# Signed bfloat16 token numbers in the dispatch table of a mixture-of-experts kernel

## The chip, the cores and the metric

The kernel runs on one core of one Trainium2 chip. The metric is the device time of one execution in microseconds (us), from a few executions of the same program on the same chip; their median is the number that counts.

## What is computed

The reference is two transformer layers with post-layernorm over x of 8 batches x 512 tokens x 512 channels, all float32:

```
x = layernorm(x + attention0(x))      # 16 causal heads of 32
x = layernorm(x + experts(x))         # 8 experts, every token goes to its best two
x = layernorm(x + attention1(x))      # 8 query heads of 64 on 2 key/value heads
x = layernorm(x + quantised_ffn(x))   # hidden size 1408, integer weights
```

The part that matters here is between the first and the second line. A router takes the softmax of 8 logits of each token and picks the best two experts, so 8 x 512 x 2 = 8192 (token, expert) pairs have to be gathered by expert, multiplied with that expert's weights, and scattered back.

## The kernel before

**Stages.** TensorE (PE) goes through four stages in the order of the layers: attention0 batch by batch, the experts tile by tile (a tile is 128 tokens of one expert), attention1 batch by batch, and the feed-forward. Stages overlap at their seams. In attention0 the loop runs over batches `b`, head groups `g` (four) and units `u` (three per group); `plan(b)` hangs side work on the slots `(g, u)`: projections of the batch itself, and for batch `b - 1` its output projection `project` (`ps_o`), its layernorm and the store of its rows to the table `rows` in DRAM, and for batch `b - 2` the routing: `choose`, `dispatch`, then at slot (1, 2) `enter(one_hot(b - 2))`. So batches 0 to 5 are entered during the loop of b = 2 to 7, and batches 6 and 7 later, between the first steps of the expert tiles. The order is written by hand for PE through attention0 and the first expert steps; the other engines' order there is found by a scheduler. From the twelfth expert tile on the order of VectorE (DVE), ScalarE (ACT), GpSimd (POOL) and of the DMA queue of SyncE (SP) is by hand as well.

**The table of tiles.** `Router.table` is 128 lanes x 256 columns; column `32 e + j` is tile j of expert e, and the entry says which token sits in that lane. It is filled by a matrix product of one-hot matrices: for each of the 4 token tiles of a batch and each of the 2 choices, `one_hot` (L574) makes a 128x128 matrix that is zero but for the token's number at (token, lane), and a 128x256 matrix that has a one at (token, column); `enter` (L591) multiplies them on PE and adds the result to the table. A bfloat16 number holds whole numbers exactly only up to 256, and a token's number goes to 4095, so it is entered in two digits, `low` (the token's place in its tile of 128) and `high` (the number of that tile): two products, 2 x 8 matrices each time, accumulated in `ps_table[:, 0]` and `ps_table[:, 1]`, and put together by DVE at L597 and L598. `matmul_by_columns` (L58) issues each product as four of 32 output lanes (`columns=32`) in the loop of attention0, and as one of 128 in the two late calls. `ps_table` is one of two rotating PSUM banks (`p_mm`), which `ps_o`, `ps_q`, `ps_k`, `ps_v`, `rs`, `ps_count` and `ps_x1T` share.

**The rows.** `layernorm` (L180) stores the normalised batch with four DMAs of 128 rows to `router.rows[512 b + 128 t]`. The expert tiles gather rows from there with an indirect DMA on POOL's queue (L863), by the numbers in the table; `load_rows` (L1941) reads a whole batch back for attention1 with one DMA of 1 MB. Batches 0 and 1 are read back during the expert tiles, in SP's hand-written order; batches 2 to 7 together when attention1 begins.

**Round trip of the expert tiles.** From tile 18 on, a pair of gathered tiles is transposed by a way through DRAM: DVE transposes 32x32 blocks, SP stores the pair (`pair<-xrT`, L902) and reads it back in another order (`xrT<-pair`, L908), four DMAs, before PE needs it.

Of the kernel before, what the change touches and what calls it, by code (L numbers as in the profile page):

```python
# [9 lines left out]
F32 = mybir.dt.float32  # L10
# [4 lines left out]
ALU = mybir.AluOpType  # L15
# [3 lines left out]
P = 128  # L19
# [14 lines left out]
TOP_K = 2  # L34

E_TILES = NB * NT


FIXED, SOON = 6, 4
# [72 lines left out]
class Env:  # L112
# [67 lines left out]
    def layernorm(self, b, dst=None):  # L180
        nc, small = self.nc, self.small
        xb = self.xs[b]
        stats = small.tile([P, NT, 6], F32, name="stats")
        mv = small.tile([P, NT, 2], F32, name="mv")
        rstd = small.tile([P, NT], F32, name="rstd")
        for t in range(NT):
            nc.vector.bn_stats(out=stats[:, t, :], in_=xb[:, t, :])  # L187
            nc.vector.bn_aggr(out=mv[:, t, :], in_=stats[:, t, :])  # L188
        nc.gpsimd.tensor_scalar(rstd, mv[:, :, 1], LN_EPS, None, ALU.add)  # L189
        nc.gpsimd.tensor_tensor(rstd, rstd, self.neg_half, ALU.pow)  # L190
        for t in range(NT):
            nc.vector.tensor_scalar(xb[:, t, :], xb[:, t, :], mv[:, t, 0:1], rstd[:, t : t + 1],  # L192
                                    ALU.subtract, ALU.mult)
            if dst is not None:
                nc.sync.dma_start(out=dst[ts(t, P), :], in_=xb[:, t, :])

    def evacuate(self, i, dst, src):
        if i % 2:
# [166 lines left out]
def quantised_ffn(env, ffn_slots):  # L365
    tc, nc, xs, vec = env.tc, env.nc, env.xs, env.vec
    with ExitStack() as phase:
        work = phase.enter_context(tc.tile_pool(name="d_work", bufs=2))
        p_gu = phase.enter_context(tc.tile_pool(name="d_gu", bufs=2, space=PSUM))
        p_o = phase.enter_context(tc.tile_pool(name="d_o", bufs=1, space=PSUM))  # L370

        sd = work.tile([P, D], F32, name="sd", bufs=1)
        nc.sync.dma_start(out=sd, in_=env.ins.s_down.partition_broadcast(P))
        env.load_ffn(ffn_slots, 6)

        n_gu = 2 * NHID
        for i, slot in enumerate(ffn_slots):
            lo, hi = UPS * i, min(UPS * (i + 1), 3 * NHID)  # L380
            cut = min(max(n_gu, lo), hi) - lo
            if cut:
                nc.vector.tensor_scalar(slot[:, :cut, :], slot[:, :cut, :].bitcast(I32), -ZERO_POINT, None, ALU.add)
            n = hi - lo - cut
            if n:
                part = slot[:, cut : cut + n, :]
                nc.vector.scalar_tensor_tensor(part, part.bitcast(I32), -ZERO_POINT,
                                               sd[:, None, :].to_broadcast([P, n, D]), ALU.add, ALU.mult)

        def wf(u):  # L390
            return ffn_slots[u // UPS][:, u % UPS, :]

        for b in range(NB):
            xb = xs[b]
            x3T = work.tile([P, ND, S], F32, tag="x3T", name="x3T")
            env.transposed(x3T, xb, p_gu, "g")
            os = [p_o.tile([P, D], F32, tag=f"o{t}", name=f"ps_f{t}") for t in range(NT)]

            def ffn_out(c, hT):
                for t in range(NT):  # L400
                    nc.tensor.matmul(os[t], lhsT=hT[:, ts(t, P)], rhs=wf(n_gu + c), start=c == 0, stop=c == NHID - 1)

            before = None
            for c in range(NHID):
                g = p_gu.tile([P, S], F32, tag="g", name="ps_g1")
                u = p_gu.tile([P, S], F32, tag="u", name="ps_u1")
                for ps, w in ((g, wf(2 * c)), (u, wf(2 * c + 1))):
                    for dc in range(ND):
                        nc.tensor.matmul(ps, lhsT=w[:, ts(dc, P)], rhs=x3T[:, dc, :], start=dc == 0, stop=dc == ND - 1)
                sg = work.tile([P, S], F32, tag="sg", name="sg1")  # L410
                nc.scalar.activation(sg, g, AF.Silu, scale=vec[:, V_SG + c : V_SG + c + 1])
                hT = work.tile([P, S], F32, tag="hT", name="hT2", bufs=3)
                nc.vector.scalar_tensor_tensor(hT, u, vec[:, V_SU + c : V_SU + c + 1], sg, ALU.mult, ALU.mult)
                if before is not None:
                    ffn_out(c - 1, before)
                before = hT
            ffn_out(NHID - 1, before)
            for t in range(NT):
                nc.vector.tensor_tensor(xb[:, t, :], os[t], xb[:, t, :], ALU.add)
            env.layernorm(b, env.ins.out[b])  # L420

class Router:
# [4 lines left out]
    def __init__(self, env, keep, pool, small, tmp, dram):  # L429
        nc = env.nc  # L430
        self.env, self.nc, self.keep, self.small = env, nc, keep, small
        self.results = dram.tile([(N_FIXED + N_FREE) * P, D], F32, name="results")
        self.rows = dram.tile([NB * S, D], F32, name="rows")
        n = NB * NT
        self.hots = pool.tile([P, TOP_K, n, E], F32, name="r_hots")
        self.weights = keep.tile([P, TOP_K, n], F32, name="r_weights")
# [29 lines left out]
        self.tiles = numbers("r_tiles", [N_FREE], [[1, N_FREE]])  # L466
        i = tmp.tile([P, 1], I32, name="r_lane_i")
        nc.gpsimd.iota(i, pattern=[[0, 1]], base=0, channel_multiplier=1)
        self.lane = pool.tile([P, 1], F32, name="r_lane")
        nc.vector.tensor_copy(self.lane, i)  # L470
        i = tmp.tile([P, S], F32, tag="r_inv", name="r_columns_i", bufs=2)[:, : E * E_TILES].bitcast(I32)
        nc.gpsimd.iota(i, pattern=[[1, E * E_TILES]], base=0, channel_multiplier=0)
        self.columns = pool.tile([P, E * E_TILES], BF16, name="r_columns")
# [100 lines left out]
    def one_hot(self, b, room, tiles):  # L574


        nc, n = self.nc, TOP_K * NT
        room = room.rearrange("p c t -> p (c t)").bitcast(BF16)
        low = room[:, : n * P].rearrange("p (i l) -> p i l", l=P)
        high = room[:, n * P : 2 * n * P].rearrange("p (i l) -> p i l", l=P)  # L580
        column = room[:, 2 * n * P :].rearrange("p (i l) -> p i l", l=E * E_TILES)
        lanes = self.columns[:, :P]
        for k, t in ((k, t) for t in tiles for k in range(TOP_K)):
            i, lane = TOP_K * t + k, self.to_lane[:, k, t : t + 1]
            nc.vector.tensor_scalar(low[:, i, :], lanes, lane, self.lane, ALU.is_equal, ALU.mult)
            nc.vector.tensor_scalar(high[:, i, :], lanes, lane, float(NT * b + t), ALU.is_equal, ALU.mult)
            nc.vector.tensor_scalar(column[:, i, :], self.columns, self.to_column[:, k, NT * b + t : NT * b + t + 1], None,
                                    ALU.is_equal)
        return low, high, column

    def enter(self, ps, low, high, column, columns):  # L591

        nc, n = self.nc, TOP_K * NT
        for h, part in enumerate((low, high)):
            for i in range(n):
                matmul_by_columns(nc, ps[:, h, :], part[:, i, :], column[:, i, :], i == 0, i == n - 1, columns)
        nc.vector.tensor_tensor(self.table, ps[:, 0, :], self.table, ALU.add)  # L597
        nc.vector.scalar_tensor_tensor(self.table, ps[:, 1, :], float(P), self.table, ALU.mult, ALU.add)  # L598

    def soon(self, pool, ps, held):  # L600

# [216 lines left out]
class Tiles:  # L818
# [39 lines left out]
    def fetch(self, i, room=None):  # L858
        if i < self.n:
            self.xrs[i] = xr = self.work.tile([P, D], F32, tag="xr", name="xr", bufs=6) if room is None else room  # L860

            n = (NB - 2) * S if i < self.n_soon else NB * S
            self.nc.gpsimd.indirect_dma_start(  # L863
                out=xr, out_offset=None, in_=self.router.rows[:n],
                in_offset=bass.IndirectOffsetOnAxis(ap=self.tokens(i), axis=0))
# [270 lines left out]
class IntegerFfn:  # L1136
# [102 lines left out]
    def batch(self, b):  # L1239
# [15 lines left out]
        if not final:  # L1255
            for t in range(NT):
                self.out(os, t, NHID - 1, parts[NHID - 1])
            for t in range(NT):
                self.scaled(b, os, t)
            env.layernorm(b, env.ins.out[b])  # L1260
            return

        order = [(t, c) for ts_ in ((0, 1), (2,), (3,)) for cs in (range(hold, NHID - 1), (NHID - 1,)) for t in ts_ for c in cs]
# [20 lines left out]
def attention0(env, guard, keep, routes, experts, dram, p_mm, tiles_ctx):  # L1284
# [8 lines left out]
    with ExitStack() as phase:  # L1293
# [37 lines left out]
        router = Router(env, keep, routes, small, work, dram)  # L1331
        router.load()
        load_x(0)

        for i in range(N_FIXED + N_FREE - RARE, N_FIXED + N_FREE):
            nc.sync.dma_start(out=router.results[ts(i, P), :], in_=guard.total)
# [48 lines left out]
        def project(b, t, out_of_heads=False):  # L1385
            ps = mm([P, D], "ps_o")
            for c in range(ND):
                (wide if out_of_heads else multiply)(ps, aoTs[b][:, c, ts(t, P)], wo[:, c, :], c)
            nc.vector.tensor_tensor(xs[b][:, t, :], ps, xs[b][:, t, :], ALU.add)
            if t == NT - 1:  # L1390
                env.layernorm(b, router.rows[S * b : S * (b + 1)])

        x1Ts, logits = {}, {}

# [45 lines left out]
            return router.one_hot(b, rooms[b], places)  # L1440

        def enter(rows, mm=mm, columns=HD):
            router.enter(mm([P, 2, E * E_TILES], "ps_table"), *rows, columns)

        def scores(b, g, u):
            q, k = heads[b, g]
# [481 lines left out]
def usual_pass(tc, ins, held_out):  # L1928
    nc = tc.nc
    with ExitStack() as ctx:  # L1930
# [4 lines left out]
        with tc.tile_pool(name="a_mm", bufs=2, space=PSUM) as p_mm, ExitStack() as attn1_ctx:  # L1935
            with tc.tile_pool(name="routes", bufs=1, side="right") as routes, \
# [2 lines left out]
                router, tiles, tables = attention0(env, guard, keep, routes, experts, dram, p_mm, tiles_ctx)  # L1939

                def load_rows(b):  # L1941
                    rows = router.rows[S * b : S * (b + 1)]
                    nc.sync.dma_start(out=env.xs[b], in_=rows.rearrange("(t p) d -> p t d", p=P))
# [333 lines left out]
```

## Time and profile before

| | |
|---|---|
| time, median of 3 executions | 2129.05 us (2126.14 to 2129.59) |
| the profiled execution, its time | 2131.2 us |
| its span, first to last instruction | 2129.5 us |
| PE busy | 2088.1 us, 98% of the span |
| DVE busy | 1278.1 us, 60% |
| ACT / POOL busy | 607.0 us, 29% / 497.9 us, 23% |
| granted TensorE clock, mean | 0.998 of full speed |
| HBM read and written | 129.96 MB and 75.76 MB, 97 GB/s over the span |

Busy time of an engine counts its instructions, overlapping ones once. The profiled execution is 2.15 us above the median of the three, and 1.7 us of its time lie outside its span. A line of a timeline gives the start, the duration, the engine, the source line, the operation with `output<-inputs`, and in brackets how long the engine was idle before and what ended that. On PE several entries of one duration overlap, since matmuls are pipelined.

### The profile page before, as it was taken

The numbers are of one execution on the slowest core, as the hardware profiler recorded it, in microseconds if no ns is written. First come the engines' busy times: TensorE is split into PE (matmuls) and PEld (weight loads), VectorE is DVE, ScalarE is ACT, GpSimd is POOL, SyncE is SP. The second block draws the span as 40 slices with busy tenths as digits, with TensorE's granted clock in tenths as the row PEclk, the third lists the DMA queues.
The fourth block names the chain that finished last, engine by engine and source line by source line (L and its number), as shares of the span: only waits on it lengthen the run. The fifth ranks groups of instructions, "written<-read, shape, count | busy, mean of one in ns | idle before, by whom it ended". The sixth has DMA issues, their size and how long they took to land. (4 is left out here: it accounts for less than half of the span.)

```text
span 2129.5 us, 36298 instructions
## 1 busy us (share of the span) xinstructions
PE 2088.1 (98%) x15322; PEld 1056.4 (50%) x15322; DVE 1278.1 (60%) x2015; ACT 607.0 (29%) x838; POOL 497.9 (23%) x489
## 2 busy tenths in 40 slices
PE   8999999999998999999999999999999999999997
PEld 2333333333333677775433333333334888888886
DVE  2667676676767644224237898888867644555443
ACT  2333323323333111111133333333332232222222
POOL 2343534334342211232042312322101000000000
PEclk9999999999999999999999999999999999999999
DMA  9020303415232337787651312132101311111000
GB/s 321 21 74 28 100 7 115 137 53 159 67 114 100 124 124 231 219 236 214 176 203 55 99 50 90 60 100 68 52 1 60 95 53 60 60 60 60 20 21 21
DMA packets 170444, 208.16 MB, mean 98 GB/s; under 512 B 61714, under 2 KB 114962, under 8 KB 167202
## 3 DMA queue, kind: packets, MB, share of 16 engines
q1 hardware_dynamic: 158992, 170.08, 25.8%
q0 software_dynamic: 10560, 34.61, 5.5%
q8 instruction: 123, 2.02, 0.4%
q10 hardware_dynamic: 722, 1.07, 0.1%
q14 instruction: 47, 0.39, 0.1%
HBM read 129.96 MB, written 75.76 MB: 97 GB/s over the span
## 5 line engine op out<-in xcount | busy, mean ns | idle before, releaser
L1460 ACT ACTIVATE p<-sc 128x2048 f32<-128x2048 f32 (+1 forms) x96 | 153.0, 1593 | 185.4 <-PE sc L62 161.8
L1068 POOL TENSOR_TENSOR g_total<-g_total,r_inv 128x512 f32<-128x512 f32 x64 | 90.1, 1408 | 491.0 <-DVE r_inv L1838 270.0
L1495 DVE TENSOR_TENSOR p<-p 128x1536 f32<-128x1536 f32 (+2 forms) x96 | 149.5, 1558 | 81.3 <-POOL p L1470 78.0
L1218 DVE SCALAR_TENSOR_TENSOR hT<-ps_u,vec,sg 128x512 f32<-128x512 f32 x88 | 65.5, 744 | 189.1 <-PE ps_u L1213 189.0
L1229 PE MATMUL ps_f<-ffn_w,h_half 128*128 128x512 f32 x672 | 169.9, 393 | 2.5 <-DVE h_half L1224 1.9
L948 PE MATMUL ps_gu<-xrT,experts 128*128 128x256 f32 x736 | 166.7, 380 | 1.0 <-DMA xrT<-pair 1.0
L948 PEld LDWEIGHTS ps_gu<-xrT,experts 128*128 128x128 f32 x736 | 138.9, 190 | 33.4 <-issue 15.1
L1808 ACT ACTIVATE p<-sc 128x1024 f32<-128x1024 f32 x128 | 124.7, 1022 | 98.2 <-PE sc L62 98.0
L1838 DVE RECIPROCAL r_inv<-r_inv 128x512 f32<-128x512 f32 x32 | 107.1, 3346 | 68.3 <-ACT r_inv L1065 68.3
L1229 PEld LDWEIGHTS ps_f<-ffn_w,h_half 128*128 128x128 f32 x672 | 124.4, 188 | 34.8 <-DVE h_half L1224 7.5
L1213 PE MATMUL ps_g<-x_high,ffn_w 128*128 128x512 f32 x352 | 137.3, 390 | 0.9 <-DVE x L1780 0.9
L1213 PE MATMUL ps_u<-x_high,ffn_w 128*128 128x512 f32 x352 | 137.1, 389 | 0.0
L1213 PE MATMUL ps_g<-x_low,ffn_w 128*128 128x512 f32 x352 | 137.0, 389 | 0.0
L1213 PE MATMUL ps_u<-x_low,ffn_w 128*128 128x512 f32 x352 | 137.0, 389 | 0.0
L62 PE MATMUL sc<-qT,kT 64*64 64x512 f32 x1024 | 124.7, 602 | 2.4 <-issue 1.3
L62 PE MATMUL ps_q<-experts 128*32 128x512 f32 x1024 | 121.5, 603 | 4.9 <-DMA experts<-in_xT 4.5
L1470 POOL TENSOR_SCALAR_AFFINE_SELECT p<-p 128x512 f32<-128x512 f32 x128 | 81.9, 652 | 167.7 <-ACT p L1460 161.1
L62 PE MATMUL ps_v<-experts 128*32 128x512 f32 x1024 | 120.9, 595 | 0.0
L1827 PE MATMUL av<-p,v 128*64 128x512 f32 x512 | 120.9, 594 | 0.0
L62 PE MATMUL ps_o<-attn_out,aoT 128*64 128x512 f32 x512 | 116.4, 598 | 0.8 <-ACT r_inv L1065 0.8
L62 PE MATMUL ps_k<-experts 128*32 128x512 f32 x1024 | 116.3, 594 | 0.0
L62 PE MATMUL ps_q<-hT,attn_qkv 128*64 128x512 f32 (+1 forms) x504 | 116.2, 596 | 0.0
(276 smaller groups left out, 3222.0 us busy)
## 6 DMA issues: line engine op xcount, KB each, us to landing
results<-y SPq DMA_DIRECT2D x68, 256.0 KB
turned<-turned SPq DMA_DIRECT2D x56, 256.0 KB
pair<-xrT SPq DMA_DIRECT2D x25, 512.0 KB
xrT<-pair SPq DMA_DIRECT2D x100, 128.0 KB
x<-in_x SPq DMA_DIRECT2D x8, 1024.0 KB
rows<-x SPq DMA_DIRECT2D x32, 256.0 KB
x<-rows SPq DMA_DIRECT2D x8, 1024.0 KB
experts<-in_xT SPq DMA_DIRECT2D x7, 1024.0 KB
```

What stands on the lines that cost most here:

```text
L62: nc.tensor.matmul(out[m], lhsT=lhsT[:, m], rhs=rhs, start=start, stop=stop)
L948: nc.tensor.matmul(ps[:, j, :], lhsT=w, rhs=xT[:, c, :], start=c == 0, stop=c == ND - 1)
L1068: self.nc.gpsimd.tensor_tensor(self.total, self.total, r_inv, ALU.add)
L1213: nc.tensor.matmul(ps, lhsT=w[:, ts(dc, P)], rhs=x[:, dc, :], start=(dc, i) == (0, 0), stop=(dc, i) == (ND - 1, 1))
L1218: nc.vector.scalar_tensor_tensor(hT, u, vec[:, V_SU + c : V_SU + c + 1], sg, ALU.mult, ALU.mult)
L1229: self.nc.tensor.matmul(os[t], lhsT=h[:, ts(t, P)], rhs=self.weights(2 * NHID + c), start=(c, i) == (0, 0), stop=(c, i) == (NHID - 1, 1))
L1460: nc.scalar.activation(p, sc[:, :, :width], AF.Exp, scale=scale)
L1470: nc.gpsimd.affine_select(out=first, in_=first, pattern=[[0, 4], [1, P]], compare_op=ALU.is_ge, fill=0.0, base=0, channel_multiplier=-1)
L1495: nc.vector.tensor_tensor(total[:, :, P * kt :], total[:, :, P * kt :], p[:, :, at : at + w], ALU.add)
L1808: nc.scalar.activation(p, sc, AF.Exp, scale=scale)
L1827: nc.tensor.matmul(st["av"][HD * j : HD * (j + 1), :], lhsT=st["v"][:, kt, HD * j : HD * (j + 1)], rhs=p[:, j, :], start=kt == 0, stop=kt ...
L1838: nc.vector.reciprocal(r_inv, r_inv)
```

## The change

A token enters the table as one number. Within a batch the token's number less 256 goes from -256 to 255; numbers from 0 on are raised by one, so that none is zero: -256 to -1 and 1 to 256, all exact in bfloat16. `held` is `513 b + 256` wherever the product isn't zero, and table + product + held is the token's row in DRAM. So that no decoding is needed, `rows` has 513 rows per batch, the one in the middle (number 256) unused. That row is written once with zeros, because the gather's range covers it. The value `held` is kept in the room in SBUF that `high` had. Tile t of a batch begins at `row_at(b, t)`; as the two halves of a batch no longer touch, `load_rows` takes two DMAs of 512 KB in place of one of 1 MB.

```
+GAP = S // 2
...
-                nc.sync.dma_start(out=dst[ts(t, P), :], in_=xb[:, t, :])
+                nc.sync.dma_start(out=dst(t), in_=xb[:, t, :])
...
-        self.rows = dram.tile([NB * S, D], F32, name="rows")
+        self.rows = dram.tile([NB * (S + 1), D], F32, name="rows")
...
+        self.signed = pool.tile([P, NT], F32, name="r_signed")
+        for t in range(NT):
+            nc.vector.tensor_scalar(self.signed[:, t : t + 1], lane, float(P * t - GAP + (P * t >= GAP)), None, ALU.add)
...
         for k, t in ((k, t) for t in tiles for k in range(TOP_K)):
             i, lane = TOP_K * t + k, self.to_lane[:, k, t : t + 1]
-            nc.vector.tensor_scalar(low[:, i, :], lanes, lane, self.lane, ALU.is_equal, ALU.mult)
-            nc.vector.tensor_scalar(high[:, i, :], lanes, lane, float(NT * b + t), ALU.is_equal, ALU.mult)
+            nc.vector.tensor_scalar(token[:, i, :], lanes, lane, self.signed[:, t : t + 1], ALU.is_equal, ALU.mult)
             nc.vector.tensor_scalar(column[:, i, :], self.columns, self.to_column[:, k, NT * b + t : NT * b + t + 1], None,
                                     ALU.is_equal)
...
-        for h, part in enumerate((low, high)):
-            for i in range(n):
-                matmul_by_columns(nc, ps[:, h, :], part[:, i, :], column[:, i, :], i == 0, i == n - 1, columns)
-        nc.vector.tensor_tensor(self.table, ps[:, 0, :], self.table, ALU.add)
-        nc.vector.scalar_tensor_tensor(self.table, ps[:, 1, :], float(P), self.table, ALU.mult, ALU.add)
+        for i in range(n):
+            matmul_by_columns(nc, ps, token[:, i, :], column[:, i, :], i == 0, i == n - 1, columns)
+        nc.vector.tensor_scalar(held, ps, 0.0, float((S + 1) * b + GAP), ALU.not_equal, ALU.mult)
+        nc.vector.tensor_tensor(self.table, ps, self.table, ALU.add)
+        nc.vector.tensor_tensor(self.table, held, self.table, ALU.add)
+
+    def row_at(self, b, t):
+        return (S + 1) * b + P * t + (P * t >= GAP)
...
-            n = (NB - 2) * S if i < self.n_soon else NB * S
+            n = (NB - 2 if i < self.n_soon else NB) * (S + 1)
...
+        nc.sync.dma_start(out=router.rows[GAP :: S + 1], in_=guard.total[:NB, :])
...
-            router.enter(mm([P, 2, E * E_TILES], "ps_table"), *rows, columns)
+            router.enter(mm([P, E * E_TILES], "ps_table"), *rows, columns)
...
                 def load_rows(b):
-                    rows = router.rows[S * b : S * (b + 1)]
-                    nc.sync.dma_start(out=env.xs[b], in_=rows.rearrange("(t p) d -> p t d", p=P))
+                    for t in range(0, NT, GAP // P):
+                        rows = router.rows[router.row_at(b, t) :][:GAP]
+                        nc.sync.dma_start(out=env.xs[b][:, t : t + GAP // P, :], in_=rows.rearrange("(t p) d -> p t d", p=P))
```

More of the change, by code (lines that the diff above doesn't have):

```diff
@@ L419, in quantised_ffn @@
                 nc.vector.tensor_tensor(xb[:, t, :], os[t], xb[:, t, :], ALU.add)
-            env.layernorm(b, env.ins.out[b])
+            env.layernorm(b, lambda t: env.ins.out[b][ts(t, P), :])
 class Router:
@@ L468, in __init__ @@
         nc.gpsimd.iota(i, pattern=[[0, 1]], base=0, channel_multiplier=1)
-        self.lane = pool.tile([P, 1], F32, name="r_lane")
-        nc.vector.tensor_copy(self.lane, i)
+        lane = pool.tile([P, 1], F32, name="r_lane")
+        nc.vector.tensor_copy(lane, i)
+        self.signed = pool.tile([P, NT], F32, name="r_signed")
+        for t in range(NT):
+            nc.vector.tensor_scalar(self.signed[:, t : t + 1], lane, float(P * t - GAP + (P * t >= GAP)), None, ALU.add)
         i = tmp.tile([P, S], F32, tag="r_inv", name="r_columns_i", bufs=2)[:, : E * E_TILES].bitcast(I32)
@@ L578, in one_hot @@
         room = room.rearrange("p c t -> p (c t)").bitcast(BF16)
-        low = room[:, : n * P].rearrange("p (i l) -> p i l", l=P)
-        high = room[:, n * P : 2 * n * P].rearrange("p (i l) -> p i l", l=P)
+        token = room[:, : n * P].rearrange("p (i l) -> p i l", l=P)
         column = room[:, 2 * n * P :].rearrange("p (i l) -> p i l", l=E * E_TILES)
+        held = room[:, n * P : 2 * n * P].bitcast(F32)[:, : E * E_TILES]
         lanes = self.columns[:, :P]
@@ L584, in one_hot, with enter @@
             i, lane = TOP_K * t + k, self.to_lane[:, k, t : t + 1]
-            nc.vector.tensor_scalar(low[:, i, :], lanes, lane, self.lane, ALU.is_equal, ALU.mult)
-            nc.vector.tensor_scalar(high[:, i, :], lanes, lane, float(NT * b + t), ALU.is_equal, ALU.mult)
+            nc.vector.tensor_scalar(token[:, i, :], lanes, lane, self.signed[:, t : t + 1], ALU.is_equal, ALU.mult)
             nc.vector.tensor_scalar(column[:, i, :], self.columns, self.to_column[:, k, NT * b + t : NT * b + t + 1], None,
                                     ALU.is_equal)
-        return low, high, column
-    def enter(self, ps, low, high, column, columns):
+        return b, token, column, held
+    def enter(self, ps, b, token, column, held, columns):
         nc, n = self.nc, TOP_K * NT
-        for h, part in enumerate((low, high)):
-            for i in range(n):
-                matmul_by_columns(nc, ps[:, h, :], part[:, i, :], column[:, i, :], i == 0, i == n - 1, columns)
-        nc.vector.tensor_tensor(self.table, ps[:, 0, :], self.table, ALU.add)
-        nc.vector.scalar_tensor_tensor(self.table, ps[:, 1, :], float(P), self.table, ALU.mult, ALU.add)
+        for i in range(n):
[5 more added lines that the diff above has]
+        return (S + 1) * b + P * t + (P * t >= GAP)
     def soon(self, pool, ps, held):
@@ L1259, in batch @@
                 self.scaled(b, os, t)
-            env.layernorm(b, env.ins.out[b])
+            env.layernorm(b, lambda t: env.ins.out[b][ts(t, P), :])
             return
@@ L1390, in project @@
             if t == NT - 1:
-                env.layernorm(b, router.rows[S * b : S * (b + 1)])
+                env.layernorm(b, lambda t: router.rows[router.row_at(b, t) :][:P])
         x1Ts, logits = {}, {}
```

## The prediction

> **What bounds the kernel now.** I read the page first: the engines' totals, and the slices.
>
> ```profile
> PE 2088.1 (98%) x15322; PEld 1056.4 (50%) x15322; DVE 1278.1 (60%) x2015; ACT 607.0 (29%) x838; POOL 497.9 (23%) x489
> PE   8999999999998999999999999999999999999997
> PEclk9999999999999999999999999999999999999999
> ```
>
> PE is busy from the first slice to the last, at a granted clock of 0.998. What leaves PE's stream shortens the run; what leaves another engine does so only where PE waits for it. So the second view is the list of PE's waits, which is short (the longest, 4.5 us, is for the first load):
>
> ```profile
> PE ps_r L62 <- DVE v L1360: 4.3, 6, 0.7
> PE av L1487 <- POOL p L1470: 4.2, 4, 1.4
> ...
> PE ps_x1T L1414 <- DVE g_routed L605: 1.6, 1, 1.6
> ...
> PE ps_gu L948 <- DMA xrT<-pair: 1.0, 1, 1.0
> ...
> PE ps_o L62 <- DVE q L1371: 0.8, 1, 0.8
> ```
>
> Columns: total us, times, longest. Two of these lie around an entry into the table (L605 and L1371, both in batch 7); L948 waits for the DMA round trip of the expert tiles. The third view is the tile `ps_table`, the timeline around one of its eight products, and the windows of two of them (length, then busy us of PE, PEld, DVE, ACT, POOL):
>
> ```profile
> L62 PE MATMUL ps_table<-one_hot x416: 272/273/273, 217.9 to 761.1; 128*32 128x256 bf16 x128, 128*128 128x256 bf16 x11
> ...
> 217.91 1.93 PE L62 MATMUL ps_table<-one_hot 128*32 128x256 bf16 x64
> 219.66 1.05 PE L1487 MATMUL av<-p,v 128*32 128x384 f32 x16
> 219.69 0.68 DVE L1389 TENSOR_TENSOR x<-ps_o,x 128x512 f32<-128x512 f32 x1
> ...
> 221.23 0.39 DVE L597 TENSOR_TENSOR r_table<-ps_table,r_table 128x256 f32<-128x256 f32 x1
> 221.68 3.64 PE L62 MATMUL ps_o<-experts,aoT 128*32 128x512 f32 x32
> ...
> 217.91:219.66 1.75, 1.75 (x69) 1.75 (x64) 1.75 (x1) 0.00 (x0) 1.75 (x2) 1.00 0.04 9
> 657.29:659.15 1.86, 1.86 (x68) 1.65 (x60) 1.86 (x3) 0.69 (x1) 1.02 (x1) 1.00 0.00 0
> ```
>
> An entry occupies PE from its first matmul to the start of the next product: 219.66 - 217.91 = 1.75 us, without a gap before or after (in the windows PE is busy for all of it). The other loop entries begin at 305.67, 392.00, 479.66 and 566.35 and take 1.75 us each too, the one of batch 7's loop 1.86 us (657.29 to 659.15), the two late ones 1.75 and 1.74 us (718.48 and 759.45). Sum: 14.1 us.
>
> **The change part by part.**
>
> *Half of the products go.* In the built program 6 x 32 matmuls of 32 lanes and 2 x 8 of 128 lanes leave PE, each with its weight load, 208 in all; nothing else on PE changes place or number. The row's price: half of the occupied time. Five loop entries in batches 2 to 6: 5 x 0.875 = 4.4 us; two late ones: 2 x 0.87 = 1.7 us; batch 7's is treated below. A rule of the Trainium skill gives another price: "TensorE: Matmul & The Clock Gate", Back-to-back issue gap, has 262 cycles for 256 columns at 2.4 GHz, 109 ns each, so 208 x 109 ns = an estimate of 22.7 us. The trace has 1.75 us / 64 = 27 ns per matmul of 32 lanes: four of them stand side by side, and only the group of four costs 109 ns. I take the trace: 7.0 us in all, not 22.7.
>
> *Does PE run into something earlier?* After the shorter product PE reaches everything behind it 0.875 us sooner, while what it needs may come when it did. Next `av` needs POOL's mask, done at 217.43: free. `sc` needs the exponential before it: free, ACT idles 6.4 us. The next `ps_o` reuses the bank that DVE empties with L1389, 219.69 to 220.37; PE now arrives at 221.68 - 0.875 = 220.81, 0.44 us later. The five are alike to 0.1 us. Everything further follows PE's own progress (the layernorm, the store, the load of the next x), so the 4.2 us of waits for POOL stay.
>
> *DVE.* Per entry 8 instructions of L586 go. In a run of one-hots they follow each other at 0.165 us (646.78 to 646.94), so 8 x 0.165 = 1.3 us; one PSUM read of 128x256 comes in (between L597 and L598, 0.39 to 0.42 us). DVE loses 0.9 us per entry, some 7 us in all, at no price and no gain where PE doesn't wait: all but batch 7. There it counts:
>
> ```profile
> 646.78 0.24 DVE L586 TENSOR_SCALAR one_hot<-r_columns,to_lane 128x128 bf16<-128x128 bf16 x1
> 646.94 0.27 DVE L587 TENSOR_SCALAR one_hot<-r_columns,r_to_column 128x256 bf16<-128x256 bf16 x1
> 647.14 0.74 DVE L1371 TENSOR_SCALAR q<-ps_q,vec 128x512 f32<-128x512 f32 x1
> 647.93 1.49 PE L62 MATMUL ps_o<-experts,aoT 128*32 128x512 f32 x12 [0.80 <-DVE q L1371]
> ...
> 663.72 0.55 PE L1414 MATMUL ps_x1T<-ident,x 128*128 128x128 f32 x3 [1.57 <-DVE g_routed L605]
> ```
>
> The one-hots hold up L1371, which empties the bank that PE wants at 647.14. 1.3 us fewer of them: the 0.80 us wait goes. Then DVE's chain from `ps_o` (651.64) over the reciprocal, four normalisations and two sums to L605 (ends 663.66) decides when PE may go on to `ps_x1T`. It begins 0.80 us earlier with PE. The scheduler also puts the table's reads ahead of the last sum (`p<-p`, 128x4x256, 1.3 us), and the bank is free after two reads of 0.4 us instead of that sum and two short ones; I get 662.7 in place of 663.66, 0.96 us. The shorter product itself is lost there, since PE would only wait longer. Batch 7: 0.80 + 0.96 = 1.8 us.
>
> *Late entries.* In the new order the table's first read stands on DVE ahead of batch 7's layernorm and waits for PE's product. That product ends at about 719.35 + 0.2, and DVE gets there at 720.1, so it doesn't wait; the layernorm comes 0.4 us later (from 721.8), 1.3 us against PE's shift, and PE wants it at 731.44. The POOL gather after the last entry has idled 14.5 us before: free.
>
> *DMAs.* Eight more on SP for `load_rows`, and one of 16 KB at the start. The latter is issued at about 12 us, behind the load of x(0), ahead of weights that PE first wants at 110.8 (`ps_o`). The six loads at attention1's start become twelve:
>
> ```profile
> 1089.72 14.42 SPq L1943 DMA_DIRECT2D x<-rows  x6
> 1104.18 2.48 SPq L1114 DMA_DIRECT2D ffn_i<-in_wq_ffn  x1
> 1106.76 2.53 SPq L1759 DMA_DIRECT2D attn_out<-in_w_attn  x2
> ```
>
> Here a rule speaks against the change: "DMA: Bandwidth & Descriptors", Rules for kernel authors, wants 1 MiB per DMA and the coalescing of transfers, and its fit gives each about 2.0 us beside its bytes; eight more would be an estimate of 16 us if exposed. The row: 6 x 1.05 MB in 14.42 us is 436 GB/s, so these issues go at the rate of the bytes, which stay the same. Even twice 14.42 us would be hidden: what stands behind on SP is wanted at 1142.33 (L1128, `ffn_i`) and 1163.48 (`attn_out`), 30 us and more after it lands. The two loads inside the expert tiles (824.92 and 855.96, 0.63 us of SP each) are followed by 1.5 us of idle SP; one more issue of 0.4 to 0.6 us fits. But the second is followed by PE's 1.01 us wait for `xrT<-pair` at 872.79, so there is no slack in that round trip; bounds -1 to +2 us, I take 0, since the bytes ahead of it are equal.
>
> *Addresses.* `r_signed` moves the tile `experts`, the gathered rows and their transposes down by 32 bytes in each partition, which are then multiples of 64. Bounds: PE's products run at 3.62 us per 16 for `ps_gu` from an address off 64, and at 1.81 per 8 for `ps_f` from one on it, the same 226 ns; I take 0.
>
> Sum: 4.4 + 1.7 + 1.8 = **7.9 us less**. The profiled execution's span of 2129.5 would become 2121.6, its time 2131.2 - 7.9 = 2123.3; it stands 2.15 us above the median, and from that, 2129.05 - 7.9 = **2121.2 us**.
>
> **The rivals.**
>
> *PE waits for what it gained.* Each DVE or DMA chain is a little later than I have it, and PE waits out the time. For it: slack at the next `ps_o` is only 0.44 us, and batch 7 shows such a chain. Against: it needs the same 0.44 us error in five like places. If L1389 came 0.9 us late, each of the five would keep nothing: 7.9 - 4.4 = 3.5 us less, 2125.5; with batch 7's 1.8 us gone as well, 2127.3. That ends inside 0.2%.
>
> *Operands at new addresses are read more slowly.* Slower than before. The place: the 736 `ps_gu` products from `xrT` and `experts`, and all of attention0 and the expert tiles, some 1060 us of PE time. The price: 1% of it is 10.6 us. It decides from 7.9 / 1060 = 0.75%, that is 379 ns to 382 ns in the row of `ps_gu`; at 1.5% the time is 2129.05 - 7.9 + 15.9 = 2137. Against it: the equal 226 ns above. The same mechanism could make them faster.
>
> *The round trip of the expert tiles.* Each split load pushes `xrT<-pair` 2 us later (the fit above): 4 us back, 2125.2. For it: the 1.01 us wait at 872.79. Against: the same bytes in the same queue.
>
> *More than I count.* DVE's 7 us less clear waits that I leave standing, such as `ps_r` (4.3) and `av` (4.2), in part: 2 to 3 us, 2118.5. Against: those waits hang on a value's evacuation and on the x load, in slots without one-hots.
>
> **How the numbers follow.** The forecast as it stands 0.62, more than I count 0.10, round trip or similar small losses 0.14, PE waits for its gain 0.08, slow addresses 0.06. About 0.2%, 4.3 us, is what a measurement can tell from no change here: faster is below 2124.8, same up to 2133.3. The forecast's own spread is the medians' (-2.9 to +0.5 us in the three runs) and the waits' 1 us: 2119 to 2123.5. Forecast and more give 0.72 faster; of the small losses most stay under 2124.8 (0.12), of the waits little (0.01): 0.85 faster. Same: 0.02 + 0.07 + 0.01 of the addresses = 0.10; slower 0.05. The range leaves out the addresses and most of the waits, and reaches to 2125.5 above and 2117.5 below.
>
> **What would show it.** `ps_table` with half its entries, 0.88 us each to the next product; no wait on L1371's successor in batch 7, the one before `ps_x1T` still there at 1 to 1.5 us; `ps_gu` at 379 ns; batches 2 to 6 each 0.88 us shorter; the feed-forward as long as before. I am wrong if PE's idle time (25.4 us now between its first and last matmul) grows by more than 2 us, if a new wait on `xrT<-pair` shows after the split loads, or if a PE row changes its duration.

## The result, and the profile after

The changed kernel takes 2119.93 us (median of 7, 2119.07 to 2123.3); the kernel before took 2129.05 us on the same chip. The medians are 9.1 us apart; the ratio on record is 0.9961, 95% interval 0.9952 to 0.9970, which is 8.3 us. Measured twice more, the ratio was 0.9969 (0.9958 to 0.9980) and 0.9954 (0.9940 to 0.9967). The mean of the three, 0.9961, is 8.2 us. The forecast was 7.9 us less, 2121.2 us.

The page first, its totals and two of its slices:

```profile
PE 2080.9 (98%) x15114; PEld 1051.5 (50%) x15114; DVE 1269.7 (60%) x1963; ACT 606.6 (29%) x838; POOL 498.2 (24%) x489
PE   9999999999999999999999999999999999999997
PEclk9999999999999999999999999999999999999999
```

PE has exactly 15322 - 15114 = 208 matmuls fewer and 7.2 us less busy time, DVE 8.4 us less. PE is as full as before: what bounds the kernel has not changed. Then the tile `ps_table` (min/median/max ns, first and last start):

```profile
L65 PE MATMUL ps_table<-one_hot x208: 272/273/273, 216.8 to 750.8; 128*32 128x256 bf16 x96, 128*128 128x256 bf16 x8
```

the timeline around the first entry,

```profile
216.75 1.06 PE L65 MATMUL ps_table<-one_hot 128*32 128x256 bf16 x32
217.63 1.05 PE L1497 MATMUL av<-p,v 128*32 128x384 f32 x16
218.08 0.68 DVE L1399 TENSOR_TENSOR x<-ps_o,x 128x512 f32<-128x512 f32 x1
...
219.41 0.41 DVE L601 TENSOR_SCALAR one_hot<-ps_table 128x256 f32<-128x256 f32 x1
...
219.65 2.78 PE L65 MATMUL ps_o<-experts,aoT 128*32 128x512 f32 x24
```

and three of the windows from the first matmul of an entry to the next product (length, then busy us of PE, PEld, DVE, ACT, POOL; last the granted clock, the DMA engines' busy share and GB/s):

```profile
216.75:217.63 0.88, 0.88 (x37) 0.88 (x33) 0.88 (x1) 0.00 (x0) 0.88 (x2) 1.00 0.00 0
648.62:649.61 0.99, 0.99 (x37) 0.77 (x29) 0.99 (x2) 0.69 (x1) 0.16 (x1) 1.00 0.00 0
709.98:710.85 0.87, 0.87 (x10) 0.79 (x8) 0.67 (x1) 0.00 (x0) 0.00 (x0) 1.00 0.00 0
```

An entry takes 0.87 us where it took 1.75, in all seven entries outside batch 7 (0.87 or 0.88). The last window is a late entry with 8 matmuls of 128 lanes, the first one with 32 of 32 lanes: the time is the same, 109 ns for one of 128 lanes or for a group of four. Nothing is waited for behind it: `ps_o` follows at 219.65, and DVE had emptied its bank (218.08 + 0.68 = 218.76) 0.9 us earlier. The second window is batch 7's, which ends at `ps_count`. Batch 7, where DVE decides, in the timeline:

```profile
638.01 0.74 DVE L1381 TENSOR_SCALAR q<-ps_q,vec 128x512 f32<-128x512 f32 x1
...
652.59 0.68 DVE L1505 TENSOR_TENSOR p<-p 128x512 f32<-128x512 f32 x1
653.18 0.41 DVE L601 TENSOR_SCALAR one_hot<-ps_table 128x256 f32<-128x256 f32 x1
653.52 0.41 DVE L602 TENSOR_TENSOR r_table<-ps_table,r_table 128x256 f32<-128x256 f32 x1
653.85 0.15 DVE L614 TENSOR_REDUCE g_routed<-ps_count 128x1 f32<-128x4 f32 x1
...
654.08 1.06 PE L1424 MATMUL ps_x1T<-ident,x 128*128 128x128 f32 x8 [1.47 <-DVE g_routed L614]
...
654.37 1.59 DVE L1505 TENSOR_TENSOR p<-p 128x1024 f32<-128x1024 f32 x1
```

The evacuation of q comes in time, and PE's 0.80 us wait for it is gone; the table's reads stand ahead of the last sum (`p<-p` 128x1024), and the wait before `ps_x1T` is 1.47 us (1.57 before), reached earlier. Laying the two PE streams over each other, PE is 7.69 us earlier than before at 601 us and 9.64 us earlier at `ps_x1T`: batch 7 brings 1.95 us. That repeats: from the product that starts at 601.95 us in the kernel before to `ps_x1T` it is 61.78 and 61.70 us in the two profiles of the kernel before and 59.82, 59.79 and 59.81 us in the three of the changed one.

In this execution not all of it lasts. Some 20 us later PE works at half its clock; the same 41 matmuls, from `sc` (the scores) to the first `ps_xrT`, in the profile of after and in that of before:

```profile
673.25:676.80 3.55, 3.55 (x41) 1.08 (x41) 2.38 (x16) 1.35 (x1) 0.66 (x1) 0.55 0.09 38
```

```profile
682.92:684.97 2.05, 2.05 (x41) 0.76 (x41) 1.87 (x13) 0.74 (x1) 0.66 (x1) 1.00 0.08 26
```

The clock records have 0.50 for 3.4 us from 673.1 us on, behind a wait of `sc` of 2.5 us. The 41 matmuls take 1.50 us longer, a shorter wait behind them gives some back, and PE's lead is 8.50 us at 678 us. Such a stretch stands at this place in eight of the fourteen profiles of this document, although `sc` waits 2.5 to 3.0 us there in all of them: in the first and third profile of the changed kernel and not in the second, in neither profile of the kernel before, but in that of layout_alone, which has the old products. What decides it, these runs do not show, so I do not count it to the change.

The profiled execution of the changed kernel has a span of 2118.1 us, 11.4 less than the one of before. The entries and batch 7 explain 5 x 0.875 + 2 x 0.87 + 1.95 = 8.1 of these. The rest, 3.3 us, is PE's lead at 601 us beyond its five shorter entries (7.69 - 4.38); behind 601 us the half clock, two waits that went or shrank (`xrT<-pair` and the one at attention1's start) and the tail of the execution nearly cancel. It lies in waits such as that of `av` (probabilities times values) for POOL's mask. Whether those belong to the change is the first thing that the experiments had to settle.

### The profile page after: what moved, and what is told of

The parts are those of the page before. It is cut to its first block, busy times and chain, and to the rows that moved or that the text cites. A ratio compares the mean times of both kernels' runs of the same rounds, so it can differ in the third digit from the quotient of the medians.

```text
span 2118.1 us, 35841 instructions
## 1 busy us (share of the span) xinstructions
PE 2080.9 (98%) x15114; PEld 1051.5 (50%) x15114; DVE 1269.7 (60%) x1963; ACT 606.6 (29%) x838; POOL 498.2 (24%) x489
## 5 line engine op out<-in xcount | busy, mean ns | idle before, releaser
L957 PEld LDWEIGHTS ps_gu<-xrT,experts 128*128 128x128 f32 x736 | 139.2, 191 | 31.9 <-issue 15.6
```

What stands on the lines that cost most here:

```text
L957: nc.tensor.matmul(ps[:, j, :], lhsT=w, rhs=xT[:, c, :], start=c == 0, stop=c == ND - 1)
```

## The experiments

### Two more profiles of each kernel: which waits belong to the change

The kernel before, again:

> The kernel before, unchanged, for a second profile. Theory (the change took PE work and batch 7's DVE chain, nothing else): the eight waits that both profiles show at different lengths (av on POOL's mask 4.2 us before and 2.8 after, xrT<-pair 1.0 and none, sc at 1099 us 1.3 and none) are luck of one execution, and here they come out differently again; the seven 1.75 us entries and the waits 0.80 (ps_o) and 1.57 (ps_x1T) of batch 7 repeat to 0.05 us. Rival (the change itself shortens those waits): they repeat at 4.2, 1.0 and 1.3 us.

The changed kernel, again, twice:

> The changed kernel, unchanged, for a second profile and an anchor on this chip. Theory: 7.9 us under the kernel before, ratio 0.9963; entries 0.87 us, the wait before ps_x1T 1.47 us again; the av, xrT<-pair and sc waits anywhere between those of the two first profiles. Rival: av again 2.8 us, xrT<-pair and sc again none, ratio 0.9950 to 0.9957.

> The changed kernel as an anchor beside the three kernels that follow, and for a third profile. Theory: ratio to the kernel before 0.9963; 0.87 us per entry, 1.47 us before ps_x1T; the waits of av on POOL's mask and the wait at attention1's start have again another length.

PE's waits in the second profile of the kernel before:

```profile
PE rs L1835 <- DVE total L1816: 1.6, 1, 1.6
PE av L1487 <- POOL p L1470: 1.0, 2, 0.6
...
PE ps_o L62 <- DVE q L1371: 0.7, 1, 0.7
```

and in the second and third of the changed one:

```profile
PE av L1497 <- POOL p L1480: 4.5, 6, 1.5
...
PE sc L65 <- issue: 1.5, 1, 1.5
PE ps_x1T L1424 <- DVE g_routed L614: 1.5, 1, 1.5
```

```profile
PE av L1497 <- POOL p L1480: 5.4, 6, 1.6
...
PE rs L1845 <- DVE total L1826: 1.0, 1, 1.0
```

`av` on POOL's mask took 4.2 and 1.0 us in the two profiles of before, 2.8, 4.5 and 5.4 in the three of after (the last two above the range that after_again expected): no gain of the change. The second profile of before is of a single execution of 2126.46 us, below all 23 others on that chip. The wait for `xrT<-pair` (1.0 us) is absent from the second profile of before, so it was not the change that took it away. The wait at attention1's start (`sc` or `rs`, the scores or the row sums of the probabilities) was 1.3, 1.6, 0.4, 1.5 and 1.0 us. What repeats to within 0.1 us is what the forecast counted: 1.75 or 0.87 us per entry, 0.7 to 0.8 us of `ps_o` in the old kernel alone, 1.57 and 1.47 us before `ps_x1T`. The other 3.3 us of the first pair of profiles were luck of those two executions; why these waits vary was not found.

### PE's part and DVE's part by themselves

The second product back, read by nobody (`ps_table` again with two halves; run pe_back):

```
+        for h in range(2):
+            for i in range(n):
+                matmul_by_columns(nc, ps[:, h, :], token[:, i, :], column[:, i, :], i == 0, i == n - 1, columns)
+        ps = ps[:, 1, :]
```

> The changed kernel with its product made twice, the first of the two read by nobody: PE has as many matmuls as before the change, VectorE the changed kernel's work. Theory: five entries at 0.875 and two late ones at 0.87 us come back, 6.1 us over the changed kernel; batch 7's own second product costs nothing, the wait before ps_x1T shrinks from 1.47 to 0.6 us. Rival (PE waits out what it gains): less than 3 us come back. Second rival (each matmul is worth 109 ns): 22.7 us come back.

Measured: 2129.19 us, ratio to the kernel before 0.9997 (0.9988 to 1.0006); the changed kernel on the same chip had 2122.66. So 6.5 us come back, and with PE's matmuls the whole gain is no longer measurable. 6.5 us for 208 matmuls is 31 ns each, not 109, and some of that is batch 7's order. The expectation for batch 7 was wrong, though. The longer product did not hide in the wait:

```profile
657.50 2.00 DVE L1507 TENSOR_TENSOR p<-p 128x512 f32<-128x512 f32 x2
659.42 0.42 DVE L603 TENSOR_SCALAR one_hot<-ps_table 128x256 f32<-128x256 f32 x1
...
660.32 1.07 PE L1426 MATMUL ps_x1T<-ident,x 128*128 128x128 f32 x8 [1.93 <-DVE g_routed L616]
```

Both sums (x2) stand ahead of the table's reads again, as before the change; presumably the scheduler, with the longer product, saw the table ready later. The wait is 1.93 us where I expected 0.6, so batch 7's product was not free but cost 1.3 us (61.14 us from the product above to `ps_x1T`, for 59.8). With the seven other entries, 6.1 us, that makes 7.4 us by the profile for 6.5 by the medians, a difference within their spread. So of batch 7's gain the part from the order hangs on the product's length and not on DVE's lighter load: in the next kernel DVE has the old load again, and the reads stay ahead of the last sum.

The second set of one-hots back on VectorE, read by nobody (run dve_back):

```
+            nc.vector.tensor_scalar(high[:, i, :], lanes, lane, float(NT * b + t), ALU.is_equal, ALU.mult)
```

> The changed kernel with the second set of one-hots (a tile's number at (token, lane)) made again on VectorE, 64 instructions, and read by nobody; PE has the changed kernel's stream. Theory: VectorE's time counts in batch 7 only, and there only as the wait of ps_o behind the evacuation of q: 0.8 us back, all else kept, since the table's first read stays ahead of the last sum; about 0.8 us over the changed kernel, 7 us under the one before. Rival (VectorE's lighter load is behind the shorter av and xrT<-pair waits): 3 us over the changed kernel, with av back at 4.2 us.

Measured: 2125.27 us, ratio 0.9980 (0.9971 to 0.9989), 2.6 us over the changed kernel on that chip. In the profile the wait that I named is there:

```profile
PE av L1499 <- POOL p L1482: 3.7, 5, 1.4
PE sc L65 <- ACT qT L1726: 3.5, 2, 2.8
...
PE ps_x1T L1426 <- DVE g_routed L616: 1.5, 1, 1.5
PE ps_logits L504 <- ACT p L1472: 1.2, 1, 1.2
PE ps_o L65 <- DVE q L1383: 1.0, 1, 1.0
```

`ps_o` waits 1.0 us; `av`, at 3.7, is inside its own spread, and `sc` 2.8 is the wait at attention1's start in a long form (pe_back, without these one-hots, shows the same 2.8). From the product above to `ps_x1T` it is 61.01 us, 1.2 more than in the changed kernel. That much is explained, 2.6 were measured. Two further kernels asked where the rest could be. Without the set in batch 7's loop (`if b != NB - 3:` ahead of the added line; run dve_but_7):

> dve_back, but the entry in batch 7's loop is left without the second set of one-hots, so that VectorE has them in the seven entries where PE does not wait behind them. dve_back cost 2.6 us in the medians where I expected 0.8. Theory as it was (VectorE counts in batch 7 alone): as the changed kernel, ratio 0.996 to 0.997, no wait of ps_o on q in batch 7. Rival (VectorE's one-hots cost elsewhere too, in the late entries or before the masks): ratio 0.9975 or more.

2122.07 us, ratio 0.9964 (0.9950 to 0.9977), no wait of `ps_o` on q: by the ratio that of the changed kernel (0.9954 to 0.9969 in its three measurements; it was not run beside this one). In the other seven entries DVE's one-hots are free as far as this interval tells, as the forecast had it. And four sets in batch 7's loop alone (`for _ in range(4 if b == NB - 3 else 0):`; run dve_7_x4):

> The changed kernel with four sets of unread one-hots in the entry of batch 7's loop, 32 instructions on VectorE, and none elsewhere. Theory (in batch 7 PE waits out what VectorE does ahead of q's evacuation, and nothing multiplies it): the first set makes 1.0 us of wait, as in dve_back's profile, each further one 1.3 us, 4.9 us in all over the changed kernel, seen as one wait of ps_o on q. Rival (one set in batch 7 is worth the 2.6 to 3.4 us that the medians of dve_back showed): 10 us or more over the changed kernel, with waits elsewhere than at ps_o.

2124.17 us, 2.65 us over the changed kernel's 2121.52 on that chip. PE's waits give 1.9 us at `ps_o` and 2.1 instead of 1.5 us at `ps_x1T`, 2.5 in all. The timeline of DVE shows why it is not more, and a window behind `ps_x1T` that the waits are not the whole of it:

```profile
PE ps_x1T L1427 <- DVE g_routed L617: 2.1, 1, 2.1
...
PE ps_o L65 <- DVE q L1384: 1.9, 1, 1.9
```

```profile
642.10 0.57 DVE L594 TENSOR_SCALAR one_hot<-r_columns,to_lane 128x128 bf16<-128x128 bf16 x3
642.59 0.74 DVE L1384 TENSOR_SCALAR q<-ps_q,vec 128x512 f32<-128x512 f32 x1
643.25 0.24 DVE L594 TENSOR_SCALAR one_hot<-r_columns,to_lane 128x128 bf16<-128x128 bf16 x1
```

```profile
659.90:663.30 3.40, 3.40 (x40) 2.42 (x40) 0.92 (x3) 1.99 (x3) 0.00 (x0) 0.50 0.03 7
```

Neither expectation held: 4.9 us was too much, because the scheduler moved q's evacuation into the row of one-hots (32 of the 48 stand ahead of it), and 10 us was far off. So a set in batch 7 is not worth 2.6 us. That the waits and the medians agree is partly luck: behind the two waits PE had half its clock for 3.4 us, which put it another 1.3 us behind the changed kernel's third profile, and this execution, 2125.17 us, is the slowest of its five. I hold the 1.0 us of the wait in dve_back for shown. Its difference of 2.6 us is more than noise: nine of its eleven executions took longer than the slowest of the changed kernel's seven on that chip (2124.30 us). 1.4 us of it were in no place that a profile shows twice, and stay open.

### The rows in DRAM, the addresses and the split loads

The kernel before with the new rows alone (513 per batch, the gap row, two loads per batch), and with every tile where the changed kernel has it (run layout_alone):

```
+        self.raised = pool.tile([P, NB], F32, name="r_raised")
...
-            nc.vector.tensor_scalar(low[:, i, :], lanes, lane, self.lane, ALU.is_equal, ALU.mult)
+            nc.vector.tensor_scalar(low[:, i, :], lanes, lane, lane_of(b + (P * t >= GAP)), ALU.is_equal, ALU.mult)
```

> The kernel before with the new rows alone: 513 rows per batch, the gap row written, two loads of 512 KB for each batch, and every tile in SBUF where the changed kernel has it (32 bytes lower); a token is still entered in two digits, the first raised by what the gaps before it add. PE's stream and VectorE's order are those of the kernel before. Theory (split loads, gap row and addresses cost nothing): ratio to the kernel before 1.000, within 0.0015; ps_gu stays at 379 to 380 ns. Rival, addresses: a PE row of attention0 or the expert tiles changes its duration by 1% or more, some 10 us up or down. Rival, loads: 2 to 16 us slower, with a new wait on xrT<-pair or at the beginning of attention1.

2129.72 against 2130.1 us, ratio 0.9999 (0.9990 to 1.0008). The products from the moved tiles, and from the timeline the loads at attention1's start:

```profile
L956 PE MATMUL ps_gu<-xrT,experts x736: 379/379/463, 699.6 to 962.9; 128*128 128x256 f32 x184
```

```profile
1087.63 15.59 SPq L1953 DMA_DIRECT2D x<-rows  x12
```

379 ns is the median of before to the nanosecond (min/median/max in the row), and no wait for `xrT<-pair` shows. Both rivals fall: neither the addresses nor the loads cost anything that the interval, 2 us either way, would show. To see whether split loads would ever show, four per batch (run load_in_four):

> The changed kernel with each batch's rows read back by four loads of 256 KB in place of two of 512 KB, 16 DMAs more, the same bytes. Theory: hidden, ratio to the kernel before as the changed kernel's, 0.996 to 0.997; the run of loads at attention1's start takes 15 to 20 us of SP's queue where it takes 14.8 to 15.3. Rival (a DMA's fixed cost counts: 2.0 us each by the fit in the Trainium skill, DMA: Bandwidth & Descriptors): up to an estimate of 32 us slower than the changed kernel; in a milder form the wait at attention1's start (0.4 to 2.8 us in the profiles so far) or the one for xrT<-pair grows by 2 us.

2120.62 us, ratio 0.9953 (0.9939 to 0.9967): as the changed kernel. SP's queue does take longer, but nobody waits for it; the row of the changed kernel and that of this one:

```profile
1078.22 14.75 SPq L1954 DMA_DIRECT2D x<-rows  x12
```

```profile
1079.72 20.85 SPq L1953 DMA_DIRECT2D x<-rows  x24
```

The row takes 14.36 and 14.42 us with 6 loads (two profiles), 14.21 to 15.59 us with 12 (eight profiles) and 20.85 us with 24. This is the time in which SP hands the loads over, not that in which the bytes arrive. The windows over the row of before and over that of this kernel, with the GB/s of all DMA at the end:

```profile
1089.72:1104.14 14.42, 12.46 (x78) 3.55 (x80) 5.92 (x8) 7.98 (x9) 9.24 (x9) 1.00 0.91 336
```

```profile
1079.72:1100.57 20.85, 20.22 (x122) 6.00 (x124) 13.96 (x15) 11.09 (x14) 15.70 (x14) 1.00 0.94 344
```

336 GB/s over 14.42 us are 4.8 MB, less than the 6.3 MB of the loads, so the prediction's 436 GB/s is a rate of handing over; bytes were still on their way when the row ended. The DMA engines are as busy with small loads as with large ones (0.94 and 0.91). Why the row of 24 ends later, these runs do not show.

### Three attempts at a faster version

The wait of 1.47 us before `ps_x1T` and the one at attention1's start were left standing. First, the product `ps_count` and its reading moved from slot (1, 2) to (2, 1), and the row loads of batches 3 to 7 placed in the text behind the loads of the feed-forward's weights (run soon_later_and_seam):

```
-                todo[1, 2].append(soon)
+                todo[2, 1].append(soon)
...
+            if b + 3 < NB:
+                todo[7 if first else 5].append(lambda: self.load_rows(b + 3))
```

> A version meant to be faster, on top of the changed kernel, by two waits that the profiles leave standing. One: in batch 7 the product ps_count and its reading (g_routed) come after the score of the batch before instead of right behind the table, so that ps_x1T takes a bank that ScalarE has long emptied; the wait of 1.47 us before ps_x1T should go. Two: the rows of batches 3 to 7 are read back during attention1, behind the loads of the feed-forward's weights, so that the gathers of the experts' results at attention1's start share the DMA engines with one batch's load and not with six; the wait there (0.4 to 2.8 us) should fall under 0.5. Together 2 to 3 us under the changed kernel, ratio 0.995 to 0.9955. Rival: each wait only moves to the next product (x1T's second half on the table's reads, sc on its exponential), and nothing is gained: 0.9965.

2125.1 us, ratio 0.9975 (0.9964 to 0.9986): no gain. The wait only moved, to the second half of `x1T`:

```profile
PE ps_x1T L1424 <- DVE r_table L602: 1.3, 1, 1.3
...
PE rs L1845 <- DVE total L1826: 0.8, 1, 0.8
...
PE ps_x1T L1424 <- ACT x1T L1426: 0.7, 1, 0.7
```

The loads were issued from 1083.64 us on all the same, since nothing held them. So they were tied to a small memset of POOL on their buffers (run seam_held):

```
+        def hold(b):
+            nc.gpsimd.memset(xs[b][:, :: GAP // P, 0:1], 0.0)
+            self.load_rows(b)
```

> The changed kernel with the row loads of batches 3 to 7 held back into attention1, each behind a small memset of POOL on the buffer that it fills, so that they cannot be issued at attention1's start with the gathers. In the version before, they were moved in the text only and still ran from 1083.6 us on. Theory (the gathers of the experts' results share the DMA engines with this burst): the wait at attention1's start (0 to 2.8 us, 1.2 in the mean of ten profiles) goes, about 1 us under the changed kernel. Rival (the gathers are slow by themselves, 16 of them in a row on POOL's queue): the wait stays, time as the changed kernel's.

2123.67 us, ratio 0.9967 (0.9956 to 0.9978). Now the loads do come later, from 1148 us, and the wait is still there, in this execution longer than ever; SP's timeline, then PE's waits:

```profile
1081.79 0.89 SPq L1960 DMA_DIRECT2D x<-rows  x2
1148.66 0.89 SPq L1960 DMA_DIRECT2D x<-rows  x2
```

```profile
PE rs L1845 <- DVE total L1826: 3.5, 1, 3.5
...
PE ps_gu L957 <- DMA xrT<-pair: 1.8, 2, 1.0
```

So the burst of row loads is not needed for that wait, and my theory of it falls; with the loads held it was 3.5 us here and 1.6 us in the next kernel's profile. This execution is one of the slowest of its seven (2127.70 us), and behind the wait PE's clock was 0.50 for another 3.4 us, from 1099.1 us on. DVE's `total` stands there behind sums that wait for the gathered results (`yr`; DVE idles 4.27 and 3.11 us for them), and what makes those late stays open. This profile also shows the wait for `xrT<-pair` again (1.8 us), further evidence that it comes and goes by itself. Last, the whole entry of batch 7's loop behind the score, with the loads held (run late_enter_seam_held):

```
-                todo[1, 2].append(lambda: enter(one_hot(b - 2, range(NT))))
+                todo[(2, 1) if last else (1, 2)].append(lambda: enter(one_hot(b - 2, range(NT))))
```

> seam_held, and the whole entry of batch 7's loop (one-hots, product, count) moved behind the score of the batch before, so that VectorE comes to the two sums, the normalisation and then x1T without the one-hots ahead and ps_x1T without the table's bank. Theory: the waits before ps_x1T and behind it go, 1.5 us, so 2.5 us under the changed kernel. Rival: the first gather of the expert tiles, which needs the table, comes some 9 us later, and PE waits for it at ps_xrT (now at 677 us): 1 to 5 us slower.

2126.67 us, ratio 0.9986 (0.9976 to 0.9995): 5 us over the changed kernel's 2121.52. The wait before `ps_x1T` is gone, but at the new place PE catches the one-hots in the making:

```profile
661.76 3.23 PE L65 MATMUL ps_table<-one_hot 128*32 128x256 bf16 x32 [0.69 <-DVE one_hot L592]
...
664.91 0.39 PE L613 MATMUL ps_count<-r_carry,r_ones 128*128 128x8 f32 x2
```

The product waits 0.69 us and then takes 664.91 - 661.76 = 3.15 us, one-hot by one-hot, where it took 0.99. That is 0.69 + 3.15 - 0.99 = 2.85 us more, where 1.47 us were to be had. The rival with the late gather is not what shows: the `ps_xrT` of the first rows has no wait in this profile. The profile is that of the fastest of its executions (2125.23 us), and I could not follow all of the 5 us in it. Of the kernels tried, none beats the changed one beyond its interval.

## Why the prediction was right

*Half of the products.* Five entries at 0.875 and two at 0.87 us, 6.1 us: each entry lost 0.87 to 0.88 us. Made again, the product cost 6.5 us by the medians, and 7.4 us by the profile with 1.3 us for batch 7. The choice of the trace's 27 ns against 109 ns per matmul decides between 7 and 22.7 us; the measured time goes with the trace. The 109 ns are not wrong, they are the price of a group of four or of one matmul of 128 lanes (0.87 us / 8).

*Does PE run into something earlier?* No. The slack at the next `ps_o` was put at 0.44 us; it is 0.88 us in all five entries (1.31 before): the prediction left the moment at which DVE empties the bank where it was, and that moment, too, came 0.44 us sooner after the start of the entry. PE's idle time was 20.6, 23.7 and 23.4 us in three profiles (25.4 and 21.0 before).

*DVE.* 0.9 us per entry, some 7 us in all, at no price and no gain outside batch 7: DVE is busy 8.4 us less, and dve_but_7 shows no price there. *Batch 7*, 0.80 + 0.96 = 1.8 us: measured 1.95. The 0.80 was the wait on q, which came back as 1.0 us in dve_back; the 0.96 was the new order of sum and reads, which fell back in pe_back. Both steps were in the forecast, so this term was right in its mechanism too.

*Late entries.* DVE reaches the table's first read at 711.51 us without idling, as foreseen. *DMAs and addresses* at 0: layout_alone has 0.9999, and even four loads per batch are free. The zeros came true, but two of the reasons given for them do not hold. The rate of 436 GB/s is one of handing over, as shown above. And the equal 226 ns of `ps_gu` and `ps_f` compare matmuls of 256 and of 512 columns (the views give 128x256 and 128x512), so they say nothing of addresses; it is layout_alone that does. The fit of 2.0 us per DMA that speaks against the change (the Trainium skill, "DMA: Bandwidth & Descriptors", Anatomy of one DMA) is given there for DMAs that GpSimd issues; these are SP's, and no run here shows it as a price.

*The rivals.* PE waiting out its gain, slow operands and a longer round trip left no trace. "More than I count", through shorter waits of `av`, looked right in the first profile of after (2.8 us for 4.2) and is refuted by the next two (4.5 and 5.4).

The size: 9.1, 7.5 and 9.2 us were measured in the medians for 7.9. What the forecast took too lightly is the spread of executions, put at -2.9 to +0.5 us about the median from three runs; 23 runs of the kernel before on one chip reach from 2127.59 to 2133.88 about 2130.12, the waits of `av` alone differ by up to 3.2 us between two profiles of one kernel, and a stretch of half clock comes or stays away. That the agreement is as good as 1 us is in part luck.

## What to carry to other kernels

When one engine is 98% busy, price an edit by what leaves that engine's stream, and take the price from the occupied time of the group in the trace, not from a per-instruction figure: four matmuls of 32 lanes side by side cost what one of 128 lanes does. Look for the one place where another engine decides (here batch 7), and ask whether its order follows from the edit; a scheduler that sees a shorter product may reorder the rest, for better or worse. Before a difference between two profiles is explained, profile the unchanged kernel twice: of the waits that differed between the first pair, most differed as much between two executions of one kernel. And look at the granted clock behind a wait: the wait's own length need not be all that it costs.

## What was not expected of the hardware

The mean granted clock is 0.996 to 0.999 in the fourteen profiles, and yet PE ran at 0.50 for 3.4 us at a time in the middle of eight of them: behind the wait of `sc` of 2.5 us or more, in dve_7_x4 also behind waits of 1.9 and 2.1 us, in seam_held also behind one of 3.5 us. One such stretch put PE 0.8 to 1.6 us back, and it came in some executions of a kernel and not in others.

The start of attention1 had a wait of 0 to 3.5 us in the fourteen profiles, and it did not go when 5 MB of loads were taken out of its way. Splitting loads of 1 MB into halves left the time in which SP hands over 6.3 MB about where it was (14.4 us, then 14.2 to 15.6); with quarters it grew to 20.85 us, and nothing waited for it.
